# A graph kernel on one core: 45 of 512 columns of sorted sources placed by one-hot products in PSUM

## The chip, the cores and the metric

The kernel runs on one core of a Trainium2 chip. The metric is the device time of one execution in microseconds, the median of several runs. Three runs of the kernel before gave 2499.51, 2495.59 and 2485.49 us, so its median is 2495.59 us.

## What is computed

The reference takes 3125 nodes of 256 features, normalises them, and adds up three parts. The first is a message pass over 103125 edges that are sorted by destination. The second is four transformer layers with linear attention and a feed-forward part of 1024. The third is a mixture of four experts whose gates come from graph attention over 65536 other edges plus one loop per node. In outline:

```python
xn = layernorm(x)
x = x + gnn(xn, edge_attr_64, src, dst) + transformer(xn)      # 4 layers
h = layernorm(x)                                                # seen by the experts
e = leaky_relu(a_src[src2] + a_dst[dst2])                       # edge_index, 65536 edges
alpha = segment_softmax(e, dst2)
scores = mean_heads(layernorm(segment_sum(h_gat[src2] * alpha, dst2) + b_gat))
x = x + sum over the two best experts of gate * ffn_e(h)
```

The edges of the third part come unsorted. The kernel sorts them by destination first, so that softmax and sums become scans along the sorted edges. What the change touches is the last step of that sort: each edge's source number is written to the edge's place.

## The kernel before

Everything is in one function, and the engines are VectorE (DVE), ScalarE (ACT), TensorE (PE), GpSimd (POOL) and SyncE (SP), each with its own queue in order. The text of the program is one stream; a scheduler turns it into the order of each engine's queue. Instructions that have no dependency on their neighbours may move there. `tc.keep_in_program_order` and `issue_after` pin some.

*The message pass (stage A).* The 103125 edges lie in 806 columns of 128. For each column POOL issues an indirect gather of 128 rows of 256 features (`gather_chunk`, L515), and DVE adds the column before onto it wherever the destination is the same (`sum_up`, L527). Eight columns make a buffer `m_run`, of which there are three. A full buffer is stored to `run_d` by SP, and with that the next gathers may fill it. After the last column come the carries between partitions (L477 to L480), and then the sums of each node are fetched by 25 indirect gathers (`fetch`, L595) for thirteen pieces of node work (`pair`, L599 on, called pieces).

*The layers.* Beside this PE, ACT and DVE work through the four layers, in chunks of four node tiles (`keys`, `query`, `context`, `attend`, `ff_up` L1149, `ff_down` L1160). The layer code calls `pace(us)` and `beside(us)`, which advance a clock that stands for the expected time. `pace` emits one piece of node work if there is one, then the columns of the message pass that are due (`FIRST + COLUMN * columns`, with COLUMN = 1.27 us), and, once all columns are done, the sends that are due. `beside` takes jobs of the sort from a list.

*The sort of the 65536 edges.* An edge lies at partition p and column t of 128 x 512. Jobs count how many edges each destination has (`count_group`, L716), and then find each edge's place in groups of eight columns (`place_group`, with one-hot products on PE, L775 and L788). Every 32 columns (SG) `laid` writes the places as whole numbers to `place` (L687). A place is a number below 65536: 512 times the partition plus the column in the sorted order. Then `send(t)` (L805) issues one indirect DMA from POOL that scatters the 128 source numbers of column t of `pairs0` to their places in the DRAM table `by_dst`. That table was filled with the number NONE = 3199 before (L946, L947). When all 806 message columns are done, the first EARLY = 24 sends go ahead of the carries; the others follow as the clock says.

*After the layers (stage C).* `finish` normalises a chunk, computes its rows of the table `tab` (L853 to L859), stores them (L863) and scatters a part to `tgt_d` by POOL (L866), one indirect DMA per tile. When all columns are sent, `sorted_edges` loads the sorted sources `si` from `by_dst` (L928). Then POOL gathers rows of `tab_d` by `si` (L1291), 22 of 26 columns of each chunk; the other four go through one-hot products (`by_products`, L1283 and L1284). The chunks are scanned on DVE (L1356) while PE does the experts (L1408, L1419). Gates and the weighted sum end the kernel.

PSUM is divided into four pools. The pool `px` has one bank, `sums_ps`, used for counts and node ends early in the kernel and not again.

Of the kernel before, what the change touches and what calls it, by code (L numbers as in the profile page):

```python
# [8 lines left out]
F32 = mybir.dt.float32  # L9
BF16 = mybir.dt.bfloat16  # L10
I32 = mybir.dt.int32
F16 = mybir.dt.float16
AF = mybir.ActivationFunctionType
ALU = mybir.AluOpType
# [4 lines left out]
P = 128  # L19
# [10 lines left out]
TM = -(-E // P)  # L30
# [10 lines left out]
TE = E2 // P  # L41
NEXP = 4
GC = 8
GROUPS = TE // GC
SRC = 4096
# [5 lines left out]
NONE = NT * P - 1  # L51
# [8 lines left out]
def kernel(ctx: ExitStack, tc: tile.TileContext, a: dict, out: bass.AP):  # L60
    nc = tc.nc
    ctx.enter_context(nc.allow_non_contiguous_dma(reason="short vectors by partition"))
    V, S, G, T = nc.vector, nc.scalar, nc.gpsimd, nc.tensor
# [8 lines left out]
    px = ctx.enter_context(tc.tile_pool(name="px", bufs=1, space=PSUM))  # L72
# [9 lines left out]
                    base=0, channel_multiplier=-1)  # L82
    after = const.tile([P, P], F32, name="after")
    G.affine_select(out=after, in_=ones, pattern=[[-1, P]], compare_op=ALU.is_gt, fill=0.0,
                    base=0, channel_multiplier=1)
# [95 lines left out]
    so = ctx.enter_context(tc.tile_pool(name="so", bufs=1))  # L181
    mx = early.enter_context(tc.tile_pool(name="mx", bufs=1))
# [152 lines left out]
    pairs0 = so.tile([P, TE], I32, name="pairs0", tag="pairs")  # L335
# [205 lines left out]


    FIRST, COLUMN, PIECE, EARLY = 52.0, 1.27, 0.9, 24
    clock = {"now": 45.0, "columns": 0, "sent": 0}

    pieces = []

    def piece():
        if next(pieces[0], True):
            pieces.pop(0)  # L550
        clock["now"] += PIECE

    def pace(us):
        clock["now"] += us
        if pieces:
            piece()
        pinned = True
        while clock["columns"] < TM and FIRST + COLUMN * (clock["columns"] + 1) <= clock["now"]:
            sum_up(clock["columns"], pinned)
            pinned = False  # L560
            clock["columns"] += 1
            if clock["columns"] == TM:
                while clock["sent"] < min(EARLY, clock["placed"]):
                    send(clock["sent"])
                    clock["sent"] += 1
                for _ in range(len(jobs) - N_JOBS + ENDS):
                    jobs.pop(0)[1]()
                msgs.close()
                message_nodes()
        while (clock["columns"] == TM and clock["sent"] < clock["placed"]  # L570
               and FIRST + COLUMN * (TM + clock["sent"]) <= clock["now"]):
            send(clock["sent"])
            clock["sent"] += 1

# [101 lines left out]
    def laid(dst, r):  # L676

        k = r.shape[1]
        part = so.tile([P, 3, 2 * NT], F32, name="laid", tag="own_bin")
        q0, rem, a = part[:, 0, :k].bitcast(I32), part[:, 1, :k], part[:, 2, :k]  # L680
        V.tensor_scalar(q0, r, tv_inv, -0.5, op0=ALU.mult, op1=ALU.add)
        V.scalar_tensor_tensor(rem, q0, tv_less, r, op0=ALU.mult, op1=ALU.add)
        V.tensor_scalar(a, rem, tv, None, op0=ALU.is_ge)
        V.scalar_tensor_tensor(a, rem, 0.0, a, op0=ALU.is_lt, op1=ALU.subtract)
        V.tensor_tensor(a, q0, a, op=ALU.subtract)
        V.tensor_scalar(a, a, float(P), tv_gap, op0=ALU.min, op1=ALU.mult)
        V.tensor_tensor(dst, a, r, op=ALU.add)  # L687
    by_dst = dram.tile([2 * E2, 1], I32, name="by_dst")
    by_p = by_dst[:E2, :].rearrange("(p t) o -> p (t o)", t=TE)
    start_d = dram.tile([P, LO], F32, name="start_d")  # L690
# [34 lines left out]
    def split(x, near, rest):  # L725

        V.tensor_copy(near, x)
        V.tensor_tensor(rest[:, :, 0], x, near, op=ALU.subtract)

    def parts(t):  # L730
        cnt = so.tile([P, LO, GC + 1], F16, name="run", bufs=2)
        nc.sync.dma_start(cnt.rearrange("p l i -> p (l i)"), counts_d[t // GC, :, :])
        return (so.tile([P, LO], F16, name="near", bufs=3), cnt)

    def starts():
        cnt2 = so.tile([P, LO], F32, name="cnt2", tag="base")
        V.tensor_reduce(cnt2, table.rearrange("p (l i) -> p l i", i=GC + 1), AX.X, ALU.add)
        cum2 = so.tile([P, LO], F32, name="cum2", tag="oh_lo", bufs=3)
        V.tensor_tensor_scan(cum2, ones[:, :LO], cnt2, 0.0, op0=ALU.mult, op1=ALU.add)
        ps = pg.tile([P, LO], F32, name="ps_g")  # L740
        T.matmul(ps[:, :1], before, cum2[:, LO - 1:], start=True, stop=True)
        V.tensor_tensor(cum2, cum2, cnt2, op=ALU.subtract)
        base2 = so.tile([P, 1], F32, name="base2")
        V.tensor_copy(base2, ps[:, :1])
        V.tensor_scalar(cum2, cum2, base2, None, op0=ALU.add)
        nc.sync.dma_start(start_d, cum2)
        V.tensor_scalar(cum2, cum2, half, None, op0=ALU.add)
        places.append(parts(0))
        split(cum2, *places[0])

    def place_group(t):

        late = looks.pop() if looks else None
        if t < TE:
            hr = so.tile([P, GC, P], F16, name="hr", bufs=2)
            nc.sync.dma_start(hr.rearrange("p t e -> p (t e)"), row_h[t // GC:t // GC + 1, :].to_broadcast([P, P * GC]))
            ohT = ohTs[t // GC % 2]
            V.tensor_scalar(ohT[:P - 1], hr[:P - 1], bin_p[:P - 1], 2.0, op0=ALU.is_equal, op1=ALU.mult)
            ohl = low_hots(t)
            near, run_l = places.pop()  # L760
            V.tensor_tensor_scan(run_l.rearrange("p l i -> p (l i)"), goes.rearrange("p l i -> p (l i)"),
                                 run_l.rearrange("p l i -> p (l i)"), 0.0, op0=ALU.mult, op1=ALU.add)
            run = so.tile([P, GC, LO], F16, name="run_c", tag=f"counts{t // GC % 2}")
            S.copy(run, run_l[:, :, :GC].rearrange("p l i -> p i l"))
            if t + GC < TE:
                base = so.tile([P, LO], F32, name="base")
                V.tensor_tensor(base, run_l[:, :, GC], near, op=ALU.add)
                places.append(parts(t + GC))
                split(base, *places[0])

            earlier = so.tile([P, GC, P], F16, name="earlier", bufs=2)
            for i0 in range(0, GC, 4):
                ps = pt.tile([P, 4, P], F32, name="ps_t")
                for i in range(4):
                    T.matmul(ps[:, i, :], ohT[:, i0 + i, :], ohT[:, i0 + i, :], start=i == 0, stop=i == 3, skip_group_check=True)  # L775
                S.activation(earlier[:, i0:i0 + 4, :], ps, AF.Sign, bias=slope[:, 2:3], scale=slope[:, 1:2])  # L776
            looks.append((t, ohT, ohl, near, run, earlier))
        if late:
            t, ohT, ohl, near, run, earlier = late
            look = pg.tile([P, GC, LO], F32, name="ps_g")  # L780
            T.matmul(look, all_h, ohl, start=True, stop=False, skip_group_check=True)
            for k in range(3):
                for i in range(GC):
                    if k == 2:
                        a1, a2 = earlier[:, i, :], ohl[:, i, :]
                    else:
                        a1, a2 = ohT[:P - 1, i, :], run[:P - 1, i, :] if k else near[:P - 1]
                    T.matmul(look[:, i, :], a1, a2, start=False, stop=k == 2, skip_group_check=True)  # L788
            own = so.tile([P, GC, LO], F32, name="own_bin", bufs=1)
            V.scalar_tensor_tensor(own, look, float(E2), ohl, op0=ALU.add, op1=ALU.mult)  # L790
            V.tensor_reduce(number[t // SG % 2][:, t % SG:t % SG + GC], own, AX.X, ALU.add)
            if (t + GC) % SG == 0:
                V.tensor_scalar_mul(number[t // SG % 2], number[t // SG % 2], 0.5)
                laid(place[:, t + GC - SG:t + GC], number[t // SG % 2])
                clock["placed"] = t + GC

    places = []
    looks = []
    SG = 4 * GC
    number = [so.tile([P, SG], F32, name=f"number{i}") for i in range(2)]  # L800

    def send(t):

        with tc.issue_after(last_gather[0].ins):
            i = G.indirect_dma_start(out=by_dst, out_offset=bass.IndirectOffsetOnAxis(ap=place[:, t:t + 1], axis=0),  # L805
                                     in_=pairs0[:, t:t + 1], in_offset=None)
        tc.declare_no_dep(i.ins, group="by_dst", reason="each place is written once")
        tc.add_to_no_dep_group("by_dst", i.ins)
# [115 lines left out]

    def sorted_edges():

        si = so.tile([P, TE], I32, name="si", tag="oh_hi", bufs=2)
        tc.keep_in_program_order(nc.sync.dma_start(si, by_p))  # L928
        edges.update(si=si)

    NCH = HG + H4
# [770 lines left out]
```

## Time and profile before

One profiled execution took 2499.97 us; its span, from the first to the last instruction, is 2498.3 us.

| what | value |
|---|---|
| median of three runs | 2495.59 us |
| profiled execution, its span | 2499.97 us, 2498.3 us |
| PE busy | 2047.1 us, 82% of the span |
| POOL busy | 1723.6 us, 69% |
| DVE busy | 1481.2 us, 59% |
| ACT busy | 1168.8 us, 47% |
| mean granted PE clock | 0.902 |
| sends L805, first and last start | 1198.0 and 1906.9 us, 512 of them |
| places L687 of the 16 groups of 32 columns | 559.8 to 1828.9 us |
| load of si (L928), first gather by it | 1933.7, 1939.8 us |
| last gather L1291 | 2415.3 us |

How to read it: a group's line gives the source line, the engine, the operation, output and inputs, how often, then busy time and mean ns of one, and the idle time of the engine just before these instructions with what ended it. "issue" as the reason means that the engine waited for nothing that the profile shows. In a timeline each line has the start, the length, and in brackets the idle time before it and its releaser. POOL's busy time leaves out the 0.3 us between two of its indirect DMAs, so POOL at 76% is POOL without a pause.

### The profile page before, as it was taken

The page shows a single profiled execution, that of the slowest core. Times are in us where ns is not written, and L with a number is a line of the kernel's source. Part 1 is how long each engine was busy: PE and PEld are TensorE (multiplying, and loading weights), DVE is VectorE, ACT ScalarE, POOL GpSimd, SP SyncE. Part 2 cuts the span into 40 slices and gives each one's busy share as a digit, 9 for nine tenths or more (in the row PEclk, how much of TensorE's full clock was granted, in tenths as well). Part 3 has the DMA queues.
Part 4 walks back from the last instruction along what each step waited for, and adds up shares of the span by engine and source line. Part 5 has one row for each costly group of instructions (what it writes and reads, how often), then busy time and mean ns, then how long its engine had stood idle before and what let it go on. Part 6 is the DMA issues. An engine that isn't in the chain of part 4 may idle for free. (4 is left out here: it accounts for less than half of the span.)

```text
span 2498.3 us, 32120 instructions
## 1 busy us (share of the span) xinstructions
PE 2047.1 (82%) x10045; PEld 1417.0 (57%) x10045; DVE 1481.2 (59%) x4506; ACT 1168.8 (47%) x2040; POOL 1723.6 (69%) x1755
## 2 busy tenths in 40 slices
PE   3869778587879998879499988899999698888874
PEld 2656555365556666547276665666676455555544
DVE  7886876677777667678254434656442344444446
ACT  5646555345444444444255656556544132323234
POOL 4575667667767777766777777777776766666652
PEclk9979888797889998889699989999999898999987
DMA  8986778878987877877411112213110121211112
GB/s 256 313 255 215 247 216 274 209 253 258 304 263 260 262 264 238 294 256 247 144 30 37 37 34 55 73 45 82 45 26 8 23 47 21 48 21 31 23 21 61
DMA packets 302237, 361.80 MB, mean 145 GB/s; under 512 B 183324, under 2 KB 249205, under 8 KB 288853
## 3 DMA queue, kind: packets, MB, share of 16 engines
q1 hardware_dynamic: 233061, 244.77, 30.7%
q0 software_dynamic: 68992, 114.85, 16.9%
q8 instruction: 82, 1.34, 0.2%
q14 instruction: 102, 0.84, 0.1%
HBM read 203.45 MB, written 160.11 MB: 146 GB/s over the span
## 5 line engine op out<-in xcount | busy, mean ns | idle before, releaser
L515 POOL DMA_INDIRECT m_run<-xn_d,src_i x806 | 813.8, 1010 | 378.0 <-issue 211.9
L805 POOL DMA_INDIRECT by_dst<-pairs,place x512 | 502.5, 982 | 156.1 <-issue 154.3
L527 DVE SCALAR_TENSOR_TENSOR m_run<-m_run,stay 128x320 f32<-128x320 f32 x805 | 437.6, 544 | 73.4 <-DMA m_run<-xn_d,src_i 61.9
L1291 POOL DMA_INDIRECT rows_c<-tab_d,si x340 | 326.7, 961 | 150.2 <-issue 100.4
L1149 PE MATMUL ps_a<-h,w 128*128 128x512 f32 (+1 forms) x896 | 392.6, 584 | 6.2 <-ACT h L165 6.1
L1160 PE MATMUL ps_a<-w,gT 128*128 128x256 f32 x1600 | 366.3, 383 | 0.0
L1160 PEld LDWEIGHTS ps_a<-w,gT 128*128 128x128 f32 x1600 | 304.0, 192 | 49.1 <-issue 6.1
L1149 PEld LDWEIGHTS ps_a<-h,w 128*128 128x128 f32 x896 | 168.3, 207 | 167.1 <-issue 148.7
L1150 ACT ACTIVATE gT<-ps_a,b 128x512 f32<-128x512 f32 (+1 forms) x224 | 141.0, 637 | 137.9 <-PE ps_a L1149 136.0
L124 ACT ACTIVATE hn<-xm,rstd 128x256 f32<-128x256 f32 x225 | 120.9, 594 | 62.3 <-DVE rstd L120 58.2
L776 ACT ACTIVATE earlier<-ps_t,slope 128x512 f16<-128x512 f32 x128 | 93.9, 772 | 110.8 <-PE ps_t L775 110.4
L1284 DVE SCALAR_TENSOR_TENSOR ps_g<-tile_ids,high_of,ps_g 128x500 f32<-128x500 f32 x60 | 43.8, 740 | 169.4 <-PE ps_g L1283 168.3
L1410 ACT ACTIVATE hf<-ps_a,be 128x512 f32<-128x512 f32 (+1 forms) x112 | 69.9, 640 | 154.3 <-PE ps_a L1408 147.3
L1283 PE MATMUL ps_g<-tab_c,which 128*128 128x500 f32 x120 | 69.0, 700 | 67.0 <-DVE rows_c L1286 64.3
L160 PE MATMUL ps_t<-ident,hn 128*128 128x128 f32 x450 | 83.7, 320 | 47.3 <-ACT hn L124 41.5
L1087 PE MATMUL ps_g<-xm,kr 128*128 128x256 f32 x400 | 109.6, 412 | 11.8 <-ACT kr L1085 11.3
L1061 PE MATMUL ps_a<-wq,h 128*128 128x256 f32 x400 | 100.5, 394 | 20.8 <-ACT kT L1041 12.8
L1029 PE MATMUL ps_a<-h,wk 128*128 128x512 f32 (+1 forms) x224 | 103.7, 598 | 2.7 <-ACT h L165 2.7
L1087 PEld LDWEIGHTS ps_g<-xm,kr 128*128 128x128 f32 x400 | 78.6, 205 | 44.2 <-ACT kr L1085 29.0
L160 PEld LDWEIGHTS ps_t<-ident,hn 128*128 128x128 f32 x450 | 57.5, 159 | 81.3 <-ACT hn L124 59.6
L1138 PE MATMUL ps_a<-co,hT 128*128 128x256 f32 x400 | 99.3, 391 | 0.8 <-DVE co L1129 0.6
L718 ACT CAST counts<-ps_g 128x256 f16<-128x256 f32 x64 | 80.3, 1375 | 41.5 <-PE ps_g L716 21.4
(436 smaller groups left out, 3812.4 us busy)
## 6 DMA issues: line engine op xcount, KB each, us to landing
run_d<-m_run SPq DMA_DIRECT2D x100, 1280.0 KB
m_run<-in_edge_attr_dram SPq DMA_DIRECT2D x95, 256.0 KB
hr<-row_h SPq DMA_DIRECT2D x64, 256.0 KB
m_run<-xn_d,src_i POOLq DMA_INDIRECT x806
w<-in_L_mix_W_dram SPq DMA_DIRECT2D x8, 1024.0 KB
by_dst<-pairs,place POOLq DMA_INDIRECT x512
rows_c<-tab_d,si POOLq DMA_INDIRECT x340
run_d<-rows_c SPq DMA_DIRECT2D x15, 312.0 KB
```

Of the source, the lines that this page charges most:

```text
L124: S.activation(dst, src, AF.Identity, bias=r[:, 1, i:i + 1], scale=r[:, 0, i:i + 1])
L160: T.transpose(ps[:, i * P:(i + 1) * P], src[:, c * P:(c + 1) * P], ident)
L515: last_gather[0] = G.indirect_dma_start(out=m[:, t, :D], out_offset=None, in_=xn_d, in_offset=bass.IndirectOffsetOnAxis(ap=src_i[:, t0 + t ...
L527: add = V.scalar_tensor_tensor(m[:, t, :], before_m, stay[:, c:c + 1], m[:, t, :], op0=ALU.mult, op1=ALU.add)
L805: i = G.indirect_dma_start(out=by_dst, out_offset=bass.IndirectOffsetOnAxis(ap=place[:, t:t + 1], axis=0), in_=pairs0[:, t:t + 1], in_offs ...
L1029: T.matmul(ps[:, :n], att_w[l]["wk"][:, kc, m * P:(m + 1) * P], h1[:, kc, :n], start=kc == 0, stop=kc == 1)
L1061: T.matmul(ps[:, i, :], h1[:, kc, o + i * P:o + (i + 1) * P], att_w[l]["wq"][:, kc, :], start=kc == 0, stop=kc == 1)
L1087: T.matmul(ps_x[:, m, :], kr[:, m * P:(m + 1) * P], xm[:, t, :], start=i == 0 and m == 0, stop=i == len(c) - 1, skip_group_check=True)
L1149: T.matmul(ps[:, :w], ff_w[l]["w1"][:, kc, f * P:(f + 1) * P], h2[:, kc, :w], start=kc == 0, stop=kc == 1)
L1150: S.activation(gT[:, f, :w], ps[:, :w], AF.Gelu, bias=ff_w[l]["b1"][:, f:f + 1])
L1160: T.matmul(ps[:, i, :], gT[:, f, (2 * i0 + i) * P:(2 * i0 + i + 1) * P], ff_w[l]["w2"][:, f, :], start=False, stop=f == FF // P - 1, skip_ ...
L1291: G.indirect_dma_start(out=rows_c[:, t - COLS[j], :], out_offset=None, in_=tab_d, in_offset=bass.IndirectOffsetOnAxis(ap=si[:, t:t + 1], a ...
```

## The change

The first three columns of every group of 32, except in the last group, are no longer scattered by POOL: 3 x 15 = 45 of 512. For each of them two one-hots are built on DVE: one over 128 partitions that marks the high part of the place, and one over 512 columns that marks the low part and carries the source number, shifted to be symmetric about zero and without a zero. A product of the two, one f16 matmul with 128 x 512 outputs, adds 128 sources at their places into the one bank `sums_ps`; all 45 add up there. After the load of `si`, which holds NONE at those places, one addition on DVE puts the sources in. The digits of three columns are worked out together (`addressed`: two whole-number operations, a cast, a comparison and a combination). `pace` emits at most one product per call (`post`). The count of the clock is adapted, so that the later sends are emitted earlier by the columns saved. A constant of 512 numbers (`places`) is added on POOL; the list that had that name is renamed `starts_of`.

In the order of the built program, the queue of POOL loses 45 scatters and gains one iota and is otherwise the same: 21 instead of 24 scatters stand ahead of the carries, and between the fetches of node sums stand as many scatters as before. PE gains 45 weight loads and 45 products, DVE 45 x 2 one-hots, 15 x 5 preparing operations and four at the end, ACT one copy.

```diff
     FIRST, COLUMN, PIECE, EARLY = 52.0, 1.27, 0.9, 24
-    clock = {"now": 45.0, "columns": 0, "sent": 0}
+    clock = {"now": 45.0, "columns": 0, "sent": 0, "by_pe": 0}
...
         if pieces:
             piece()
+        if by_pe:
+            post()
...
         while (clock["columns"] == TM and clock["sent"] < clock["placed"]
-               and FIRST + COLUMN * (TM + clock["sent"]) <= clock["now"]):
+               and FIRST + COLUMN * (TM + clock["sent"] - clock["by_pe"]) <= clock["now"]):
+            clock["by_pe"] += sent_by_pe(clock["sent"])
             send(clock["sent"])
             clock["sent"] += 1
...
+    places = mx.tile([P, TE], F16, name="places")
+    G.iota(places, pattern=[[1, TE]], base=0, channel_multiplier=0, allow_small_or_imprecise_dtypes=True)
...
+    SENT_BY_PE, MID = 3, SRC // 2 - 486
+    by_pe, posted = [], []
+
+    def sent_by_pe(t):
+        return t % SG < SENT_BY_PE and t < TE - SG
+
+    def addressed(t0):
+        n = SENT_BY_PE
+        pl, sr = place[:, t0:t0 + n], pairs0[:, t0:t0 + n]
+        digit = mx.tile([P, 2, n], I32, name="post_i", bufs=2)
+        f = mx.tile([P, 4, n], F32, name="post_f", bufs=2)
+        V.tensor_single_scalar(digit[:, 0, :], pl, 9, op=ALU.logical_shift_right)
+        V.tensor_single_scalar(digit[:, 1, :], pl, TE - 1, op=ALU.bitwise_and)
+        V.tensor_copy(f[:, :2, :], digit)
+        V.tensor_scalar(f[:, 2, :], sr, MID + 0.5, None, op0=ALU.is_lt)
+        V.scalar_tensor_tensor(f[:, 3, :], sr, float(-MID), f[:, 2, :], op0=ALU.add, op1=ALU.subtract)
+        by_pe.extend((f, k) for k in range(n))
+
+    def post():
+        if not posted:
+            posted.append(px.tile([P, TE], F32, name="sums_ps"))
+        f, k = by_pe.pop(0)
+        hot = so.tile([P, P + TE], F16, name="post_hot", tag="oh_hi", bufs=2)
+        V.tensor_scalar(hot[:, :P], places[:, :P], f[:, 0, k:k + 1], None, op0=ALU.is_equal)
+        V.tensor_scalar(hot[:, P:], places, f[:, 1, k:k + 1], f[:, 3, k:k + 1], op0=ALU.is_equal, op1=ALU.mult)
+        posted.append(T.matmul(posted[0], hot[:, :P], hot[:, P:], start=len(posted) == 1,
+                               stop=len(posted) == SENT_BY_PE * (TE // SG - 1), skip_group_check=True))
+
     def send(t):
 
+        if sent_by_pe(t):
+            if t % SG == 0:
+                addressed(t)
+            return
         with tc.issue_after(last_gather[0].ins):
...
     def sorted_edges():
 
+        while by_pe:
+            post()
+        pd = posted[0]
+        here = [so.tile([P, TE], F32, name="posted", tag="earlier", bufs=2) for _ in range(2)]
+        S.copy(here[1], pd)
+        V.tensor_scalar(here[0], here[1], 0.0, float(NONE - MID), op0=ALU.is_equal, op1=ALU.mult)
+        V.scalar_tensor_tensor(here[1], here[1], 0.0, here[1], op0=ALU.is_lt, op1=ALU.add)
+        V.scalar_tensor_tensor(here[0], here[1], float(MID - NONE), here[0], op0=ALU.add, op1=ALU.add)
         si = so.tile([P, TE], I32, name="si", tag="oh_hi", bufs=2)
         tc.keep_in_program_order(nc.sync.dma_start(si, by_p))
+        V.tensor_tensor(si, si, here[0], op=ALU.add)
         edges.update(si=si)
```

More of the change, by code (lines that the diff above doesn't have):

```diff
@@ L747, in starts @@
         V.tensor_scalar(cum2, cum2, half, None, op0=ALU.add)
-        places.append(parts(0))
-        split(cum2, *places[0])
+        starts_of.append(parts(0))
+        split(cum2, *starts_of[0])
     def place_group(t):
@@ L759, in place_group @@
             ohl = low_hots(t)
-            near, run_l = places.pop()
+            near, run_l = starts_of.pop()
             V.tensor_tensor_scan(run_l.rearrange("p l i -> p (l i)"), goes.rearrange("p l i -> p (l i)"),
@@ L767, in place_group @@
                 V.tensor_tensor(base, run_l[:, :, GC], near, op=ALU.add)
-                places.append(parts(t + GC))
-                split(base, *places[0])
+                starts_of.append(parts(t + GC))
+                split(base, *starts_of[0])
             earlier = so.tile([P, GC, P], F16, name="earlier", bufs=2)
@@ L795, in place_group @@
                 clock["placed"] = t + GC
-    places = []
+    starts_of = []
     looks = []
```

## The prediction

> **What bounds the kernel now.** I read the page first, then busy time by stage, then the timeline at the seams. In the page's list of groups two lines matter:
>
> ```profile
> L515 POOL DMA_INDIRECT m_run<-xn_d,src_i x806 | 813.8, 1010 | 378.0 <-issue 211.9
> L805 POOL DMA_INDIRECT by_dst<-pairs,place x512 | 502.5, 982 | 156.1 <-issue 154.3
> ```
>
> A send (L805) costs POOL 0.98 us and 0.30 us between two: 1.26 us. The question is whether POOL's time in that stage is anybody's time. The stages, in busy us of each engine (columns: window, width, PE, PEld, DVE, ACT, POOL, granted clock, DMA share, GB/s):
>
> ```profile
> 540.00:1198.00 658.00, 551.67 (x3036) 393.79 (x3036) 488.18 (x1312) 304.03 (x519) 478.66 (x477) 0.90 0.81 268
> 1198.00:1236.00 38.00, 6.02 (x44) 3.30 (x42) 5.14 (x13) 4.05 (x6) 26.99 (x27) 0.63 0.41 110
> 1236.00:1933.00 697.00, 648.12 (x3410) 457.35 (x3411) 330.12 (x1087) 392.08 (x700) 521.50 (x532) 0.94 0.17 43
> ```
>
> Stage A (to 1198 us) is the message gathers: POOL issues almost without pause and the DMA engines are 81% busy. Stage B (1236 to 1933) is the sends beside layers 2 and 3: PE is busy 648 of 697 us. Between them lies a hole of 38 us in which PE does nothing; the timelines of POOL and PE say why:
>
> ```profile
> 1196.48 1.21 POOL L515 DMA_INDIRECT m_run<-xn_d,src_i  x1 [0.30 <-issue]
> 1198.00 1.00 POOL L805 DMA_INDIRECT by_dst<-pairs,place  x1 [0.30 <-issue]
> ...
> 1228.74 1.61 POOL L480 DMA_INDIRECT run_d<-over,carry_i  x1 [0.30 <-issue]
> 1233.67 1.00 POOL L595 DMA_INDIRECT aggr<-run_d,sum_i  x1 [3.32 <-DMA run_d<-over,carry_i]
> ```
>
> ```profile
> 1236.67 0.88 PE L611 MATMUL ps_t<-ident,aggr 128*128 128x128 f32 x3 [31.52 <-DMA aggr<-run_d,sum_i]
> ```
>
> The first 24 sends stand on POOL ahead of the carries, and PE, ACT and DVE all wait for what follows them. These sends are on the path. Where stage B ends, POOL's timeline shows:
>
> ```profile
> 1906.85 0.96 POOL L805 DMA_INDIRECT by_dst<-pairs,place  x1 [0.30 <-issue]
> ...
> 1923.26 0.97 POOL L866 DMA_INDIRECT tgt_d<-tab,start_i  x1 [0.30 <-issue]
> 1933.51 0.95 POOL L866 DMA_INDIRECT tgt_d<-tab,start_i  x1 [9.28 <-DVE tab L859]
> ...
> 1938.54 0.98 POOL L1250 DMA_INDIRECT first_row<-tab_d,d  x1 [0.30 <-ACT low_t L1268]
> 1939.83 0.96 POOL L1291 DMA_INDIRECT rows_c<-tab_d,si  x1 [0.30 <-issue]
> ```
>
> The last send is issued at 1907, POOL works off thirteen tgt scatters, and then idles 9.28 us for the last chunk's tab, which PE's layer chain delivers. So the later 488 sends are not on the path: the PE chain is later by 9.3 us. From 1940 on, POOL's 340 gathers (L1291) carry stage C, which the change hardly touches.
>
> **The change part by part.** Durations are the profiled execution's, whose own time is 2499.97 us (span 2498.3); it lies 0.18% over the runs' median 2495.59.
>
> *Removed.* 15 groups of 32 columns lose 3 sends each: 45 x 1.26 = 57 us of POOL. Three are among the first 24 (columns 0 to 2): 3 x 1.26 = 3.8 us come out of the hole, on the path. The other 42 only make POOL earlier where it already waits for PE. Even that is partly lost, since sends need place (L687):
>
> ```profile
> 1627.60 0.19 DVE L687 TENSOR_TENSOR place<-laid,number 128x32 int32<-128x32 f32 x1
> ```
>
> ```profile
> 1650.73 0.96 POOL L805 DMA_INDIRECT by_dst<-pairs,place  x1 [0.30 <-issue]
> ```
>
> This is the place of columns 320 to 351 and the first send that uses it: 23 us apart. With 30 sends fewer before it POOL is there 38 us earlier, and waits 15. For columns 352 on (place 1688.2, send 1691.8 before, 33 fewer) it waits another 23. So POOL ends its sends 57 - 38 = 19 us earlier. What is queued behind these waits is sends and tgt scatters only: the last aggr fetch is at 1580. Value of the 42 sends: 0. The stall that is late next is the same one, tab L859.
>
> *Added on PE.* 45 weight loads and 45 f16 matmuls of 512 columns. The nearest row is the bf16 matmul of 65x512 (L1157), and what matters is when the next one starts:
>
> ```profile
> 1911.42 0.38 PE L1157 MATMUL ps_a<-b_parts,ones_b 65*128 65x512 bf16 x1
> 1911.64 7.07 PE L1160 MATMUL ps_a<-w,gT 128*128 128x256 f32 x32
> ```
>
> 0.22 us each. In the built order of the changed kernel, which I set against the times of the trace, the products do not stand with the sends: 24 of 45 lie between 590 and 1185 us, soon after their place, and 21 between 1310 and 1790. The first 24 (5.3 us) are hidden, because PE reaches the hole with 31.5 us to spare; without that cover they would cost all 5.3. The other 21 fall into the stage that PE sets: 4.6 us.
>
> *Added on DVE.* Two tensor_scalars for each product and five small operations for each group. Nearest row:
>
> ```profile
> L758 DVE TENSOR_SCALAR ohT<-hr,bin_p 127x1024 f16<-127x1024 f16 x64 | 31.8, 496 | 20.4 <-DMA hr<-row_h 16.7 <-PE ps_g L788 3.0 <-PE ps_t L775 0.6
> ```
>
> Small operations there take 0.18 to 0.19 us, so 512 wide is about 0.18 + (0.50 - 0.18)/2 = 0.34, 128 wide 0.22, a product 0.56 and a group's preparation 5 x 0.19 = 0.95. Stage A gets 24 x 0.56 + 8 x 0.95 = 21 us, stage B 21 x 0.56 + 7 x 0.95 = 18 us.
>
> In A the additions stand in front of the running sums (L527), which free the buffers that the gathers fill:
>
> ```profile
> POOL m_run L515 <- DVE m_run L527: 24.1, 13, 5.9
> ```
>
> (waits of POOL from 540 to 1198: 24.1 us in 13 stops.) Bounds are 0 and 21 us. Carrying each addition along DVE's recorded timeline until an idle gap swallows it, something is left at four of POOL's stops: 1.2, 2.1, 1.2 and 0.7, together 5 us. I take 4, since those gaps move as well.
>
> Here a rule speaks against the change. The Trainium skill, page "SBUF — State Buffer", section "Who interferes with whom", says that a tensor_scalar in a two-port mode holds the port pair that GpSimd needs to write descriptors, and that the loser blocks fully. The trace has such meetings:
>
> ```profile
> 1299.59 1.32 POOL L805 DMA_INDIRECT by_dst<-pairs,place  x1 [0.30 <-issue]
> ```
>
> ```profile
> 1300.00 0.48 DVE L758 TENSOR_SCALAR ohT<-hr,bin_p 127x1024 f16<-127x1024 f16 x1
> ```
>
> This send lasted 1.32 instead of 0.96. Counted over stage A, though, the 33 gathers beside an L758 are 98 ns longer than 950 ns on average, and the 297 beside an L527, which is nearly always there, are 86 ns longer. By the rule at its full length the 48 new tensor_scalars would cost POOL 24 x 0.56 = 13 us; by the row 48 x 0.04 (half of 86, as they push an L527 aside) = 2 us. I take 2. Together A costs 4 + 2 = 6 us, bounds 0 and 34.
>
> In B, DVE is only 47% busy, but the one-hots have two buffers: the third of a group waits for the first product, and in PE's order the three mostly stand next to each other, so PE waits for about one pass over DVE (0.56 and two handovers). The trace shows no such wait; the nearest rows are PE's waits for gh L638, 4.4 us in 7. Bounds: 0 and 7 groups x 1.5 = 10. I take 3 us.
>
> *Once.* The iota of 512 (about half of L355's 1.94 us) lies before POOL's first wait of 29.5 us: 0. Copying out the bank and three operations of 512 on DVE stand near 1827 us, where DVE is half idle: 0. The addition to si (0.69 us, as L1163) comes after si lands (1936.4), and POOL is ready for its first gather at 1939.8, so the four tgt scatters hide it; if it came through it would cost 0.7. I take 0.4, for the chain of products of the first chunk behind it.
>
> **Sum.** 6.0 - 3.8 + 4.6 + 3.0 + 0.4 = +10.2 us: 2510 against the profiled 2500, or 2495.6 x 2510.2/2500 = 2505.8, say 2505 us. That is +0.4%, inside 0.5%, about what a measurement of this kernel can tell from no change. The change moves 57 us off an engine that was waiting, onto the two that it waited for.
>
> **Rivals.** *Sends set the end of stage B* in the runs that are timed. For: POOL's slack is only 9.3 us, and the runs before spread over 14. Against: the wait for tab L859 is there, and the waits for place leave 19 us at most. It would give 2495.6 - 19 + 6 = 2483. Chance 0.11.
>
> *DVE stands still inside A* (the slower side). The third one-hot, queued in front of L527, waits for a product that stands behind other work on PE; PE's longest run of feed-forward matmuls there is 13.8 us (L1149, at 1107.7). It decides once such a wait is longer than DVE's next idle gap and the ring of three buffers is empty, as at POOL's 13 stops. By the built order the product is due 1.4 to 11 us ahead, so most waits are short. Eight groups at 4 us: +32 in place of 4, so 2495.6 + 38 = 2534. Chance 0.25.
>
> *Everything hides* and only the 3.8 us remain: 2492. Chance 0.12. My forecast, 0 to +12 us, has 0.42; a dearer B (10 in place of 3 us, and the port at the rule's 13) gives 2523, chance 0.10.
>
> **How the numbers follow.** Faster by over 0.5% (below 2483) is the first rival (its 2483 pays all of A's cost; with less of it the time is lower) and some drift between runs: 0.12. Slower by over 0.5% (above 2508) is the second rival, the dear B, and little of my own case: 0.38. The rest, 0.50, is no change. The range reaches from the first rival to the second, 2483 to 2536.
>
> **What would show it.** In the profile of the changed kernel: L805's successor 467 times; the hole on PE at the end of A 27 to 28 us instead of 31.5; POOL waiting for place L687 by some 38 us in total and for tab L859 by more than 9.3 before the last tgt scatters; the last message gather 3 to 9 us later than 1196.5; PE from the first aggr transpose to the last tab longer by some 8 us than 697; stage C unchanged within 2 us. The prediction is wrong if POOL no longer waits for tab there, if DVE shows waits of several us for the new products before 1198, or if the gathers end 20 us later.

## The result and the profile after

The changed kernel takes 2503.43 us (median of 20 runs, 2494.20 to 2513.91), the kernel before, timed beside it, 2491.36 (20 runs, 2485.36 to 2503.91). The ratio is 1.0039, 95% interval 1.0027 to 1.0051: slower by 6.7 to 12.7 us. The two profiled executions hide this: 2500.38 us after (span 2498.7), 2499.97 before. That of before lies above its kernel's median and that of after below its own, so the traces are compared stage by stage here, and the times are taken from the timed runs.

First the page's list of groups, of the changed kernel (busy us and mean ns of one, then the idle time in front):

```profile
L842 POOL DMA_INDIRECT by_dst<-pairs,place x467 | 461.9, 989 | 177.6 <-issue 139.9
L515 POOL DMA_INDIRECT m_run<-xn_d,src_i x806 | 815.1, 1011 | 375.3 <-issue 211.5
```

POOL is rid of 45 sends and 41 us of busy time, 54 us with the gaps between them. The message gathers have kept their length: 1011 ns for 1010. The same windows as before the change (columns: window, width, PE, PEld, DVE, ACT, POOL, granted clock, DMA share, GB/s):

```profile
540.00:1198.00 658.00, 560.02 (x3118) 397.28 (x3116) 506.54 (x1418) 308.51 (x527) 482.87 (x479) 0.91 0.83 269
1198.00:1236.00 38.00, 9.75 (x51) 6.41 (x51) 5.15 (x13) 4.46 (x9) 27.00 (x29) 0.64 0.48 127
1236.00:1933.00 697.00, 645.20 (x3427) 453.45 (x3425) 346.07 (x1169) 391.55 (x697) 481.73 (x488) 0.96 0.17 42
```

In stage B POOL has 40 us less work, DVE 16 more. PE has 3 us less although products were added: the clock that it was granted is 0.96 in place of 0.94. The seam between A and B on POOL, and PE's first operation behind it:

```profile
1195.84 0.95 POOL L515 DMA_INDIRECT m_run<-xn_d,src_i  x1 [0.30 <-issue]
1197.09 1.00 POOL L842 DMA_INDIRECT by_dst<-pairs,place  x1 [0.30 <-issue]
...
1224.05 1.61 POOL L480 DMA_INDIRECT run_d<-over,carry_i  x1 [0.31 <-issue]
1228.42 1.00 POOL L598 DMA_INDIRECT aggr<-run_d,sum_i  x1 [2.76 <-DMA run_d<-over,carry_i]
```

```profile
1232.03 1.64 PE L614 MATMUL ps_t<-ident,aggr 128*128 128x128 f32 x6 [25.14 <-issue]
```

From the last gather to the carries it is 28.2 us where it was 32.3: the three sends have come out of the hole. PE's idle time is 25.14 us where it was 31.52. About 4 us of that difference are the sends; the rest is that PE went idle 1.7 us later and the gathers ended 0.6 us earlier. The end of stage B:

```profile
1882.64 0.96 POOL L842 DMA_INDIRECT by_dst<-pairs,place  x1 [0.30 <-issue]
...
1904.42 0.96 POOL L903 DMA_INDIRECT tgt_d<-tab,start_i  x1 [10.73 <-DVE tab L896]
...
1918.75 0.95 POOL L903 DMA_INDIRECT tgt_d<-tab,start_i  x1 [9.58 <-DVE tab L896]
1930.92 0.96 POOL L903 DMA_INDIRECT tgt_d<-tab,start_i  x1 [11.21 <-DVE tab L896]
```

POOL sends its last column 24 us earlier (1882.6, before 1906.9), and then waits three times for tab where it waited once. POOL's waits over the whole span (us in total, times, longest):

```profile
POOL by_dst L842 <- DVE place L690: 35.9, 2, 24.6
POOL tgt_d L903 <- DVE tab L896: 31.5, 3, 11.2
```

36 us of waits for place and 22 more than before for tab make 58 us: about all that POOL was spared has come back as waiting. PE's waits for the one-hots in stage B (1236 to 1933 us) are the new item on the engine that sets the end:

```profile
PE sums_ps L832 <- DVE post_hot L831: 4.3, 4, 2.3
```

**How the stages stand once the clock is taken out.** The trace records when PE had half its clock. One such stretch in the kernel before reaches from 1208.2 to 1245.7 us. The same six products take 3.06 us inside it and 1.65 us behind it:

```profile
1238.65 3.06 PE L619 MATMUL ps_a<-wm,aT 128*128 128x256 f32 x6
1247.20 1.65 PE L619 MATMUL ps_a<-wm,aT 128*128 128x256 f32 x6
```

The 128x256 products of `ff_down` (L1160) start 427 ns apart in such stretches and 216 ns apart elsewhere. B runs from PE's first aggr transpose to the last four tgt scatters. It has 80.8 us of half clock before and 61.9 after, with PE busy for 73.1 and 57.2 of them. At full clock half of that busy time would go: 36.5 and 28.6 us. This is an estimate, since it takes all of PE's work in B to be on the path. B is 696.8 us before and 698.9 after in the traces, 660.3 and 670.3 by this estimate: +10.0.

How far one profile each can be trusted is shown by the first four experiments below. By the same estimate, the two kernels without products in B have 664.4 and 663.9 us, some 4 more than the kernel before, and the two with products in B have 668.3 and 674.2. In the mean B takes 670.9 us with products in it and 662.9 without: 8 us, with some 4 us between single profiles.

### The profile page after: what moved, and what is told of

Read it like the earlier page. It is cut to its first block, busy times and chain, and to the rows that moved or that the text cites. A ratio compares the mean times of both kernels' runs of the same rounds, so it can differ in the third digit from the quotient of the medians.

```text
span 2498.7 us, 32336 instructions
## 1 busy us (share of the span) xinstructions
PE 2051.5 (82%) x10090; PEld 1415.4 (57%) x10090; DVE 1508.2 (60%) x4675; ACT 1169.2 (47%) x2041; POOL 1683.2 (67%) x1711
## 5 line engine op out<-in xcount | busy, mean ns | idle before, releaser
L515 POOL DMA_INDIRECT m_run<-xn_d,src_i x806 | 815.1, 1011 | 375.3 <-issue 211.5
L842 POOL DMA_INDIRECT by_dst<-pairs,place x467 | 461.9, 989 | 177.6 <-issue 139.9
L527 DVE SCALAR_TENSOR_TENSOR m_run<-m_run,stay 128x320 f32<-128x320 f32 x805 | 438.8, 545 | 77.2 <-DMA m_run<-xn_d,src_i 65.2
L160 PE MATMUL ps_t<-ident,hn 128*128 128x128 f32 x450 | 83.7, 316 | 43.8 <-ACT hn L124 39.8
```

What stands on the lines that cost most here:

```text
L160: T.transpose(ps[:, i * P:(i + 1) * P], src[:, c * P:(c + 1) * P], ident)
L515: last_gather[0] = G.indirect_dma_start(out=m[:, t, :D], out_offset=None, in_=xn_d, in_offset=bass.IndirectOffsetOnAxis(ap=src_i[:, t0 + t ...
L527: add = V.scalar_tensor_tensor(m[:, t, :], before_m, stay[:, c:c + 1], m[:, t, :], op0=ALU.mult, op1=ALU.add)
```

## Experiments

The theory, P, is the prediction's: the three early sends are on the path, the other 42 are not, and the products cost stage A some 6 us through DVE and stage B some 8 us through PE. The first four kernels ran on one chip, where the kernel before took 2495.39 us (48 runs).

**The sends left out, and no products.** All 45 sends are left out, no products are made, nothing is added to si (those sources stay at the filling number).

```diff
-        if by_pe:
-            post()
...
         if sent_by_pe(t):
-            if t % SG == 0:
-                addressed(t)
             return
...
-        while by_pe:
-            post()
...
-        V.tensor_tensor(si, si, here[0], op=ALU.add)
```

> The change without its additions: the 45 scatters are left out and nothing takes their place (those sources stay at the filling number, so this part of the sort is not computed). Theory P (the prediction): three of them stand in the hole before the carries, 3 x 1.26 = 3.8 us; the other 42 only let POOL wait longer for place and tab. About -4 us, ratio 0.9985 (0.997 to 1.000). Rival S (the sends set the end of the second stage): -15 to -50 us, ratio 0.994 to 0.98. In the profile, P wants POOL to wait some 36 us for place and over 25 us for tab before the last tgt scatters.

Measured: 2485.48 us (17 runs), ratio 0.9960 (0.9948 to 0.9973), -7 to -13 us. PE and ACT have the instructions of the kernel before in the same order in this profile. Its waits of POOL:

```profile
POOL by_dst L838 <- DVE place L688: 31.5, 2, 20.5
POOL tgt_d L899 <- DVE tab L892: 24.8, 3, 11.2
```

The waits for place and tab are there without any product: it is the missing sends that make them, as P has it. B is 685.7 us in its profile, 664.4 with the clock taken out, where the kernel before has 660.3: no shorter. The hole gives 4.1 us (36.1 from the last gather to PE's transpose, before 40.2). But the time gained 10, not 4, and 0.9960 lies outside P's range (0.997 to 1.000). S (15 to 50 us) is refuted, and P is short by 3 to 9 us.

**The products made besides.** All 512 columns are sent; the 45 products are made, their sum is copied out and not added to si.

```diff
-            clock["by_pe"] += sent_by_pe(clock["sent"])
...
-        if sent_by_pe(t):
-            if t % SG == 0:
-                addressed(t)
-            return
+        if sent_by_pe(t) and t % SG == 0:
+            addressed(t)
...
-        V.tensor_tensor(si, si, here[0], op=ALU.add)
```

> All 512 scatters stay, and the 45 products with their one-hots are computed besides; their sum is copied out but not added to the sources. Theory P: the additions alone, 6 us before 1198 us and 7.6 us after the hole, about +14 us, ratio 1.0056 (1.003 to 1.008). If P's parts add up, this ratio and that of the kernel that only leaves the scatters out make the change's 1.0039. Rival S: with the sends on the path the additions after the hole are hidden behind POOL, +6 us, ratio 1.0024.

Measured: 2498.02 us (22 runs), ratio 1.0016 (1.0002 to 1.0029), +0.5 to +7 us. That is less than P's 14, and below its range (1.003 to 1.008). S's 1.0024 fits here, but S was refuted by the first experiment. POOL's waits for tab fall to a third of the 9.28 us before, so that in this profile POOL had 3.2 us to spare:

```profile
POOL tgt_d L900 <- DVE tab L893: 3.2, 1, 3.2
```

With the clock taken out B is 668.3 us, +8.0. PE's waits for the one-hots in B:

```profile
PE sums_ps L831 <- DVE post_hot L830: 0.9, 2, 0.5
```

That is 0.9 us where the changed kernel has 4.3. From about 1625 us on the scheduler has put the products elsewhere in PE's queue than in the changed kernel. The three products of group 13, for example, stand almost next to each other there (at 1745.8, 1746.1 and 1747.1 us, with none and two matmuls between them), and apart here (1773.7, 1775.0 and 1776.0 us, with 33 and 25 between). So this kernel is not quite the change's additions on top of the kernel before.

**The change for groups 8 to 14 only** (21 columns; their products stand in B, the 24 early sends stay):

```diff
-        return t % SG < SENT_BY_PE and t < TE - SG
+        return t % SG < SENT_BY_PE and 8 * SG <= t < TE - SG
...
-                               stop=len(posted) == SENT_BY_PE * (TE // SG - 1), skip_group_check=True))
+                               stop=len(posted) == SENT_BY_PE * (TE // SG - 9), skip_group_check=True))
```

> The change for the groups 8 to 14 alone, 21 columns, whose products fall after 1300 us; the first 24 sends stay whole. Theory P: 21 x 0.22 us of PE, 3 us of waits for the third one-hot and 0.4 at the end, +8 us, ratio 1.0032 (1.001 to 1.005). Rival G (all of the cost comes from the gather stage, where DVE is in the ring of buffers): 0, ratio 1.000 within 0.001.

Measured: 2509.18 us (8 runs), ratio 1.0049 (1.0027 to 1.0070), +7 to +17 us. P's 1.0032 (+8 us) lies inside, and its rival, no cost at all, is refuted. PE's waits for one-hots, all of them in B:

```profile
PE sums_ps L832 <- DVE post_hot L831: 6.5, 6, 2.5
```

**The change for groups 0 to 7 only** (24 columns; their products stand in A, three of the early sends go):

```diff
-        return t % SG < SENT_BY_PE and t < TE - SG
+        return t % SG < SENT_BY_PE and t < 8 * SG
...
-                               stop=len(posted) == SENT_BY_PE * (TE // SG - 1), skip_group_check=True))
+                               stop=len(posted) == SENT_BY_PE * 8, skip_group_check=True))
```

> The change for the groups 0 to 7 alone, 24 columns, whose products fall between 590 and 1190 us; 21 instead of 24 sends ahead of the carries. Theory P: +6 us of the gather stage less 3.8 us in the hole, +2 us, ratio 1.0009 (0.999 to 1.003). Rival G: +10 us, ratio 1.004, with the last message gather 10 us later or more waits of POOL for the running sums than the 47 us of before.

Measured: 2496.45 us (14 runs), ratio 0.9999 (0.9986 to 1.0012), -3.5 to +3 us. With 4.1 us out of the hole, A and all else then cost between 0.6 and 7 us. Early and late part together make 1.0048, which agrees with the change's 1.0039: the loss is the late part's.

The eight runs that follow can only be understood with one fact: the kernel before itself took 3654 to 3715 us in them. They ran on four chips. One of these is the chip of the first four experiments, where the same kernel had taken 2495.39 us half an hour earlier and now took 3708.58 us. PE, DVE and ACT stop for tens of us with nothing recorded that releases them. Why is not known; it was met in each of these runs over nearly three hours. From the timeline of the first of them, the kernel before with 6 early sends:

```profile
620.26 0.10 PEld L421 LDWEIGHTS <-ends_buf 128*128 128x128 f16 x1 [1.32 <-issue]
...
642.24 0.60 ACT L423 ACTIVATE ends_buf<-ps_a,above 128x403 f16<-128x403 f32 x1 [32.73 <-remote]
642.91 0.10 PEld L421 LDWEIGHTS <-ends_buf 128*128 128x128 f16 x1 [22.56 <-issue]
```

PE stands between two weight loads of one line for 22.56 us, and ACT waits with it. Single instructions keep their usual length (a gather 949 ns in the median, before 946; a 128x256 matmul 379 in both). Ratios are to the kernel before in the same condition; they say what the edits do there, and not what they would do at 2495 us.

**The kernel before with 6 early sends:**

```diff
-    FIRST, COLUMN, PIECE, EARLY = 52.0, 1.27, 0.9, 24
+    FIRST, COLUMN, PIECE, EARLY = 52.0, 1.27, 0.9, 6
```

> The kernel before with 6 instead of 24 sends ahead of the carries, nothing else. P (the prediction's picture: the early sends are on the path, the later ones are not until POOL's 9.3 us of slack at the end of stage B are used up): the hole on PE shrinks by 18 x 1.26 = 22.7 us, the 18 sends follow later, and so POOL ends its sends at the same time as now while PE's chain is due 22.7 us earlier; POOL's 9.3 us of waiting for the last tab vanish and it becomes the bound: -9 us, ratio 0.996, wait for tab below 1 us. Rival (the sends' end was never near the path): -23 us, 0.991. Rival (the hole is filled by other work, nothing to gain): 0, ratio 1.000.

Measured: ratio 0.9985 (0.9964 to 1.0005; 3708.23 us against 3715.20). In this profile the last gather and PE's transpose are 43.9 us apart.

**The changed kernel with 6 early columns**, four times, with the same edit in the changed kernel:

> The changed kernel with 6 instead of 24 columns ahead of the carries (3 sends, 3 products). P: 18 sends leave the hole, 22.7 us, and since POOL had 31 us of waits for tab at the end of stage B in the changed kernel, it is not late this time: -22 us against the changed kernel, so 1.004 - 0.009 = 0.995 of the kernel before; the hole on PE is about 5 us, the wait for tab some 5 to 15 us in all. Rival (the later sends' waits for place hold POOL to the old end): -9 us against the changed kernel, 1.000 of before, and no wait for tab.

> The same kernel as e7_after_few_early (the changed kernel with 6 instead of 24 columns ahead of the carries), wanted again because the kernel before took 3715 us on the chip of the first run, where engines pause for tens of us for no recorded reason. P, unchanged: -22 us against the changed kernel, 0.995 of the kernel before; the hole on PE is about 18 us shorter, POOL still waits 5 to 15 us for tab. Rival (the later sends' waits for place hold POOL to the old end): 1.000 of before, no wait for tab.

> Once more the changed kernel with 6 instead of 24 columns ahead of the carries, wanted where the kernel before takes its 2495 us. P, unchanged: -22 us against the changed kernel, 0.995 of the kernel before; the hole on PE is about 18 us shorter than 36, and POOL still waits 5 to 15 us for tab. Rival (the later sends' waits for place hold POOL to the old end): 1.000 of before, no wait for tab.

> The changed kernel with 6 instead of 24 columns ahead of the carries, a last time, wanted where the kernel before takes its 2495 us. P: -22 us against the changed kernel, 0.995 of the kernel before; the hole on PE is about 18 us shorter than 36, and POOL still waits 5 to 15 us for tab. Rival (the later sends' waits for place hold POOL to the old end): 1.000 of before, no wait for tab. Should the kernel before again take some 3600 us, 0.988 as in the earlier runs.

Measured: ratios 0.9899 (0.9863 to 0.9936), 0.9884 (0.9844 to 0.9924), 0.9881 (0.9832 to 0.9931), 0.9877 (0.9833 to 0.9920).

**The changed kernel with every one-hot written twice:**

```diff
-        V.tensor_scalar(hot[:, :P], places[:, :P], ...)
-        V.tensor_scalar(hot[:, P:], places, ...)
+        for _ in range(2):
+            V.tensor_scalar(hot[:, :P], places[:, :P], ...)
+            V.tensor_scalar(hot[:, P:], places, ...)
```

> The changed kernel, but both one-hots of each product are written twice (same values), the product itself once: DVE's addition of 45 x 0.66 us is doubled, PE's is not. P: what DVE's part costs comes again: about 4 us of lag in stage A and 3 to 5 us of waits for the third one-hot in stage B, so +8 us against the changed kernel, 1.007 of before, with POOL's waits for L527's successor and PE's waits for the one-hots each up by some 4 us. Rival (PE's own time is the cost, DVE has room): 0 against the changed kernel, 1.004.

Measured: ratio 0.9908 (0.9874 to 0.9942).

**42 later sends left out, no products** (as the first experiment, but group 0 is sent; the 42 columns of sources stay at the filling number), twice:

```diff
-        return t % SG < SENT_BY_PE and t < TE - SG
+        return t % SG < SENT_BY_PE and SG <= t < TE - SG
```

> The kernel before without the sends of the first three columns of groups 1 to 14 (42 of the 512; those sources stay at the filling number), the three of group 0 are sent, and there are no products and no addition. P (the later sends are off the path; 4 us of the 10 us that all 45 gave were the hole): 0, ratio 1.000 (0.998 to 1.001), with POOL's waits for place and tab as large as when all 45 were left out. Rival R (the later sends cost something all through stage B that the waits do not show, 6 us): ratio 0.9975.

> The same kernel as e9_drop_late (42 sends of groups 1 to 14 left out, those sources stay at the filling number, no products, no addition), wanted again for the same reason. P (the later sends are off the path): ratio 1.000 (0.998 to 1.001). Rival R (the later sends cost some 6 us all through stage B that the waits do not show, as the 10 us of the run without all 45 hint): ratio 0.9975.

Measured: ratios 0.9841 (0.9813 to 0.9869) and 0.9868 (0.9833 to 0.9903).

What follows from these eight. *Sends have their full price where the engines stop*: 42 of them gave 59 and 49 us, and 42 x 1.26 is 53. Neither P's 1.000 nor R's 0.9975 describes that condition. In the second of these profiles POOL waits 195.4 us in 8 stops for PE to free the aggr buffers (1.4 us in one stop in the kernel before at 2495 us), so fetches, sends and PE seem to take turns. That this is why a send is never hidden there was not tried.

*Taking sends out of the hole gave little that lasted.* In the kernel before, 18 sends (22.7 us) moved behind the carries gave 7 us (-2 to +13). In the four profiles of the changed kernel with 6 early columns the distance from the last gather to PE's transpose is 39.8, 41.9, 39.7 and 42.2 us; in the three profiles with 24 it is 64.5, 63.6 and 67.6: some 24 us less. But B is 1150, 1152, 1137 and 1147 us long against 1125.5 for the changed kernel with doubled one-hots, which has the same sends in all: 21 us longer in the mean. POOL's timeline shows what moved. First the kernel before with 6 early sends, then, for comparison, the one with 24 and 42 later sends left out:

```profile
1679.98 0.94 POOL L595 DMA_INDIRECT aggr<-run_d,sum_i  x1 [0.30 <-issue]
1681.23 0.99 POOL L805 DMA_INDIRECT by_dst<-pairs,place  x1 [0.30 <-issue]
...
1706.57 0.99 POOL L595 DMA_INDIRECT aggr<-run_d,sum_i  x1 [0.30 <-issue]
```

```profile
1706.40 0.94 POOL L596 DMA_INDIRECT aggr<-run_d,sum_i  x1 [0.30 <-issue]
1707.65 0.99 POOL L838 DMA_INDIRECT by_dst<-pairs,place  x1 [0.30 <-issue]
1708.94 0.97 POOL L838 DMA_INDIRECT by_dst<-pairs,place  x1 [0.30 <-issue]
1710.22 0.98 POOL L596 DMA_INDIRECT aggr<-run_d,sum_i  x1 [0.30 <-issue]
```

With 24 early sends two stand between the sixth and the seventh fetch of node sums, as in the kernel before at 2495 us; with 6 it is twenty, in the four profiles of the changed kernel too, and the seventh fetch starts 26.6 us after the sixth, in place of 3.8. The 18 sends have left one stretch that PE waits on and entered the next. P's -22 us for this edit left that out. At 2495 us it could not be tried.

*Whether the doubled one-hots cost anything* can't be said: the changed kernel alone was not run in this condition.

## Why the prediction was right, point by point

**The sum.** +10.2 us was put on record, +6.7 to +12.7 was measured. The sign, the size and the bound hold. That the sum comes out so near is in part luck, as far as these runs tell. Of the four experiments that take the change apart, the two by place lie inside P's ranges; the two by kind lie outside, each faster than P. And the term for stage A was not found. By its terms:

- *The hole, -3.8 us: right.* 4.1 us between last gather and carries in the changed kernel, the same in both other kernels that drop the three early sends (36.1 and 36.3 us to PE's transpose), and nothing in the two that keep them (40.1 and 40.1). (PE is busy for 6.0 of the 38 us in which the prediction says that it does nothing; its pause is the 31.5.) One thing was left out: the half clock that sets in during the hole. It reaches 9.1 us into B in the kernel before, and 3.9 and 3.4 in the changed kernel and the first experiment, worth some 3 us by the estimate above; but it reaches 9.4 us in the early part alone, which drops the three sends too.
- *The 42 later sends, 0 us: right by the traces, not quite settled by the times.* 38 us of waits for place were foreseen, 35.9 came; tab was to be waited for more than 9.3 us, it is 31.5. B is no shorter without the sends than with them (664.4 against 660.3, where single profiles differ by some 4). But the first experiment gained 6 us more than the hole explains. The mean granted clock of each timed run of these experiments is on record. In the 48 runs of the kernel before among them the time falls by 1.5 us for each 0.001 of clock (a straight line through them; 0.4 either way). The runs without the sends have 0.9077 in the mean and those of before 0.9055, so some 3 of the 6 us go with the clock. The other 3 are within what the last gather's start differs between these profiles anyway (1193.3 to 1198.8).
- *PE and the third one-hot in B, 4.6 + 3.0 us: right in kind, perhaps too small.* +10.0 with the clock taken out, 8 in the mean of three kernels with products there and three without, and 4.3 us of waits for the one-hots where 3 were put down. The plain length of B, +2.1 us against the +8 named as a sign, would have spoken against it. The late part alone cost 12 (7 to 17) where 8 was expected.
- *Stage A, 4 + 2 us: not shown.* The lag in front of the running sums does not appear in POOL's waits of 540 to 1198 us in the changed kernel:

```profile
POOL m_run L515 <- DVE m_run L527: 19.3, 17, 4.9
```

  19.3 us in 17 stops, before 24.1 in 13; the last gather came at 1195.8 us, and not 3 to 9 us later than the 1196.5 of before, as was named for a sign. By the times of the early part alone, A and all else cost 0.6 to 7 us. So the size of this term stays open; what is shown is that it is not the 30 us of the rival.
- *The port.* 30 gathers and sends beside a new one-hot in A lasted 1022 ns on average, the other 449 from 540 us on 1007: 30 x 15 ns is 0.5 us in all; in two of the other kernels it is 31 and 32 ns, 1 us. The rule of the Trainium skill (page "SBUF — State Buffer", section "Who interferes with whom"), that the loser blocks fully, would have made it 13 us; the measurement decides, and even the 2 us taken were too many.
- *One-hots.* 0.41 + 0.25 = 0.66 us for a product (medians of L831 and L830) where 0.56 was interpolated. A 128 x 512 product is recorded with 379 ns, but where another matmul follows at once, that one starts 0.22 us behind it, as was taken. A send's 0.98 and 0.30 us make 1.28; the 1.26 of the sums is the distance of their starts in the timeline, and the rest follows from it.
- *Once, 0.4 us: not seen.* The addition to si starts at 1933.9 us and lasts 0.69. POOL gathers by si first at 1937.3, behind its last tgt scatters, and nothing is recorded that waits for the addition.
- *Stage C* is 478.2 us from first to last gather, before 475.5: not within the 2 us named, but all four kernels of the first comparison have 476.3 to 479.6.

**The rivals.** Sends setting the end of B, and everything hiding: both would have been faster or even, and the interval excludes them; the waits for tab speak against the first. DVE standing still inside A: POOL's waits for L527 there did not grow, and the early part alone, with all of A's products, took as long as the kernel before. A dear B (waits of 10 us in place of 3, and the port at 13): 4.3 us of waits and 15 ns at the port speak against that size.

**What stays open.** The two halves of the change by place, late and early, add up: 1.0049 and 0.9999 against 1.0039. The two halves by kind do not: sends left out (0.9960) and products made besides (1.0016) add up to 0.9976, some 16 us away from the change (about 5 either way). The clock does not close this. At equal mean clock, by the 1.5 us for each 0.001, the sends left out give -6 us and the products besides +6 (their runs have 0.9070), together 0 where the change cost 12. The runs of the kernel before that were timed beside the change have no clock listed, so this leaves out a difference there. Two things of the traces bear on it. The products besides stand elsewhere in PE's queue, and PE waits 0.9 us for them there in place of 4.3. The scheduler also moved other instructions of PE in the changed kernel, which the first experiment leaves in their old order. The first is some 3 us by these waits; what the second costs was not measured, and the sends were not kept with the changed kernel's own order of PE. The cause is not settled. The addition to si can be left out of it, since nothing waits for it.

## What to carry to other kernels

Work taken from an engine that already waits for another comes back as waiting: ask of every saved instruction which later instruction of the same queue it brings forward, and whether that one waits for something else. By the traces only the three sends that stood ahead of the carries were worth anything here, and even such a hole can be filled only as long as what leaves it does not land ahead of the next transfer that somebody needs. Profiles of one execution differ by more than this change makes; take the granted clock out before a stage's length is used, and the size of the effect from many timed runs. An experiment that adds one half of a change is only that half if the scheduler leaves the rest in its order: compare the queues first.

## What the runs showed of the hardware

The half clock comes and goes between executions of nearly the same program: in B for 80.8, 61.9, 47.8, 56.7, 54.2 and 67.4 us in the six profiles at 2495 us, with PE busy for 42.7 to 73.1 of them, so worth up to 15 us by the estimate above, more than the change. And one chip can take 1.49 times as long for the same program half an hour later (2495 and 3709 us) at unchanged instruction lengths, with PE stopping up to 29 us and ACT up to 39 without a recorded release; there the value of an edit is another one. It was met on four chips, and its cause stayed unknown.
